# A pre-norm transformer block in f32: attention by two heads and 512 queries on tiled TensorE, projections a block behind

## Chip, cores and metric

The kernel runs on one core of a Trainium2 chip. The metric is the device time of one execution in microseconds (us), given as the median of several runs. The engines are called as in the profile: PE is TensorE (PEld its weight loads), DVE is VectorE, ACT is ScalarE, POOL is GpSimd and SP is SyncE, which here only issues DMAs.

## What is computed

`x` has shape (2, 1024, 1024): batch, tokens, features. All data is f32, there are 32 heads of 32 features, and the feed-forward width is 2752. Cut to what matters:

```python
def attn(x):
    qkv = x @ attn_qkvw + attn_qkvb               # heads of 32 features
    scores = einsum('bhqd,bhkd->bhqk', q, k) / sqrt(32)
    probs = softmax(scores, axis=-1)
    ctx = einsum('bhqk,bhkd->bhqd', probs, v)
    return ctx @ attn_ow + attn_ob
def ffn(x):
    return (silu(x @ W_gate.T) * (x @ W_up.T)) @ W_down.T
x = x + attn(layernorm(x))
x = x + ffn(layernorm(x))
```

## The kernel before

The tokens of a batch entry (S = 1024) are eight key tiles of 128 (NT) and two blocks of 512 (NS). The work has these stages: layer norm and transposes of `x` (line 259); projections of queries and keys (`qk_steps`, matmul at L366) and of values (`v_steps`, L422), whose results go to DRAM; attention by head (class `Head`); then, per block of 512 tokens, the output projection (`oproj_steps`, L711) and the feed-forward network (`ffn_steps`). The last uses the seven-product scheme for the gate and up projections (L853, 256 columns each) and for most of the down projection (L994); the sums of weights that it needs are made once by GpSimd (`weight_sum_steps`, L1105).

Attention of one head: queries and keys were stored as a rounded high part (`hi`, L379, f32r) and the rest (`lo`, L381). `load` (L465) brings them as 128 rows: for queries high, low, each twice; for keys each row in pairs, so that one f32r matmul of 128 rows forms all products of the parts. `scores(kt)` (L490) does two of these, for one key tile and all 1024 queries, into a PSUM tile `s` of two banks (two such buffers). ScalarE copies it to an SBUF tile `p` (L502), VectorE keeps a running maximum `top` over key tiles (L505, L507). `maximum` (L511) reduces it over the 128 keys and sends it through DRAM to all partitions as `m`. `less_maximum` (L545) adds the negative maximum to `p`, on GpSimd for six of eight key tiles and VectorE for two. `exponential` (L548) is ScalarE's. `values(kt)` (L550) multiplies `p` by `vones`, which are the 32 features of the values beside 32 columns of ones, so that contexts and softmax sums arise together: two matmuls of 64 weight columns, the first 512 queries into PSUM rows 0 to 63 and the second into rows 64 to 127. They come in runs of four key tiles (RUN). `finish` copies `acc` and stores contexts and sums to DRAM; `prep_ctx` takes reciprocals and multiplies contexts by them, on GpSimd (L660).

What sets the order is a planner, the class `Emitter` (L44). Steps carry costs in planner nanoseconds (`MM4` = 855 for an f32 matmul of 512 columns, `MM1` = 230 for an f32r one). `run(fill, paced, side)` takes steps of two lists: a paced step marked as a beat goes out when it is due, beats being spread evenly over the cost of both lists, and fill steps stand between; a step can need a mark that another gives, and `later` puts off a step by planner time (loads, stores and the maximum's way through DRAM use it). Side steps go out as soon as their needs are met. Each engine executes its instructions in the order in which they are emitted.

Attention's beats are key tiles: at beat `n` the scores of tile `n`, the subtraction of tile `n-10`, the exponential of tile `n-11` and, every fourth beat, four `values` up to tile `n-12`. `p` has RING = 16 buffers. The main part (L1206 to L1219) makes two long lists: the first runs 32 heads and two more heads' scores beside the projections of both batch entries (`fill`), the second runs the rest beside the last projections (`keep_qk`) and the output projection and feed-forward network of batch entry 0 (`ffn0`). The feed-forward network of entry 1 (`ffn1`) has no attention beside it. Thirty matmuls are cut from the end of `ffn0` (`keep`) and run after attention has ended.

Of the kernel before, what the change touches and what calls it, by code (L numbers as in the profile page):

```python
# [130 lines left out]
def preln_block_kernel(  # L131
# [28 lines left out]
    MM4, MM1 = 855.0, 230.0  # L160
    QTR = 4
    LAG = 2
    RUN = 4
    RING = NT + LAG + RUN + 2
# [44 lines left out]
    def dtile(shape, name):  # L209
        return dram.tile(shape, F32, tag=name, name=name)  # L210

    dq = {
        (b, g, w): dtile([P, 2, S], f"dq{b}_{g}_{w}")
        for b in range(B)
        for g in range(G)
        for w in range(2)
    }
    dv = {(b, hf): dtile([S, NH], f"dv{b}_{hf}") for b in range(B) for hf in range(NHF)}
    dctx = {(b, i): dtile([H // QTR, S], f"dctx{b}_{i}") for b in range(B) for i in range(QTR)}
    dsum = {(b, i): dtile([HEADS // QTR, S], f"dsum{b}_{i}") for b in range(B) for i in range(QTR)}  # L220
    drec = {(b, i): dtile([HEADS // QTR, S], f"drec{b}_{i}") for b in range(B) for i in range(QTR)}

# [128 lines left out]
    def qk_steps(q, b, g, halves=None):  # L351
# [5 lines left out]
        def store(w, s, hl, part):  # L357
            rows = dq[b, g, w][:, hl, s * NH : (s + 1) * NH]
            nc.sync.dma_start(rows, part.bitcast(F32))

        def project(w, s, kc):
            if kc == 0:
                qk_ps[w, s] = lps(f"pq_{b}_{g}_{w}_{s}")
            ps = qk_ps[w, s]
            hk, k = divmod(kc, KC // 2)
            nc.tensor.matmul(  # L366
                ps,
                wqk[b, g, w, hk][:, k, :],
                xnT[b, s][:, kc, :],
                start=(kc == 0),  # L370
                stop=(kc == KC - 1),
            )
            if s == NS - 1 and k == KC // 2 - 1:
                wst.next()
            if kc < KC - 1:
                return
            bias = bqk_t[:, w * G + g : w * G + g + 1]
            hi = Sm(f"hi_{b}_{g}_{w}_{s}", F32R)
            nc.scalar.activation(hi, ps, AF.Identity, bias=bias, scale=1.0)  # L379
            lo = Sm(f"lo_{b}_{g}_{w}_{s}", F32R)  # L380
            nc.vector.scalar_tensor_tensor(lo, ps, bias, hi.bitcast(F32), ALU.add, ALU.subtract)  # L381
            last = w == 1 and s == NS - 1
            em.later(4000.0, lambda: store(w, s, 0, hi))
            em.later(5500.0, lambda: store(w, s, 1, lo), ("qk", b, g) if last else None)
# [61 lines left out]
    vones = [const.tile([P, NT, 2, HD], F32, tag=f"vones{i}", name=f"vones{i}") for i in range(2)]  # L446
    for t in vones:
        nc.gpsimd.memset(t[:, :, 1, :], 1.0)
# [5 lines left out]
    class Head:  # L454
# [3 lines left out]
        def __init__(self, b, h):  # L458
            self.b, self.h, self.g = b, h, h // HPG
            self.hf = self.g // (G // NHF)  # L460
            self.name = f"{b}_{h}"
            self.v = vones[(b * HEADS + h) % 2]
            self.p = {}

        def load(self, i):  # L465


            if i == 0:
                self.qk = [
                    att.tile([P, S], F32R, tag=tag, bufs=2, name=f"{tag}_{self.name}")  # L470
                    for tag in ("qs", "ks")
                ]
            r = (self.h % HPG) * HD
            src = dq[self.b, self.g, min(i, 1)][r : r + HD, :, :]
            if i == 0:
                twice = bass.AP(src.tensor, src.offset, [[S, 2 * HD], [0, 2], [1, S]])
                nc.scalar.dma_start(self.qk[0].bitcast(F32), twice)
            else:
                part = src[:, i - 1, :]
                twice = bass.AP(part.tensor, part.offset, [part.ap[0], [0, 2], part.ap[1]])  # L480
                nc.scalar.dma_start(self.qk[1][i - 1 :: 2, :].bitcast(F32), twice)

        def load_v(self):
            c = (self.h * HD) % NH
            nc.sync.dma_start(
                self.v[:, :, 0, :],
                dv[self.b, self.hf][:, c : c + HD].rearrange("(c p) n -> p c n", p=P),
            )

        def scores(self, kt):  # L490
            q, k = self.qk
            ps = psum.tile([P, S], F32, tag="s", bufs=2, name=f"s_{self.name}_{kt}")
            for s in range(NS):
                nc.tensor.matmul(  # L494
                    ps[:, s * NH : (s + 1) * NH],
                    k[:, kt * P : (kt + 1) * P],
                    q[:, s * NH : (s + 1) * NH],
                    start=True,
                    stop=True,
                )  # L500
            p = self.p[kt] = Pt(f"p_{self.name}_{kt}")
            nc.scalar.copy(p, ps)  # L502
            if kt == 1:
                self.top = att.tile([P, S], F32, tag="top", bufs=1, name=f"top_{self.name}")
                nc.vector.tensor_tensor(self.top, ps, self.p[0], ALU.max)  # L505
            elif kt > 1:
                nc.vector.tensor_tensor(self.top, ps, self.top, ALU.max)  # L507
            if kt == NT - 1:
                self.maximum()

        def maximum(self):  # L511
# [15 lines left out]
            def turn():  # L527
# [11 lines left out]
                ("max", self.b, self.h),  # L539
            )  # L540

        def less_maximum(self, kt):
            p = self.p[kt]
            eng = nc.vector if kt % 4 == 3 else nc.gpsimd
# [4 lines left out]

        def values(self, kt):  # L550

            if kt == 0:
                self.acc = psum.tile([P, NH], F32, tag="acc", bufs=1, name=f"acc_{self.name}")
            for s in range(NS):
                nc.tensor.matmul(  # L555
                    self.acc[s * 2 * HD : (s + 1) * 2 * HD, :],
                    self.v[:, kt, :, :].rearrange("p a n -> p (a n)"),
                    self.p[kt][:, s * NH : (s + 1) * NH],
                    start=(kt == 0),
                    stop=(kt == NT - 1),  # L560
                )
# [3 lines left out]
        def finish(self):  # L565
            part, n = divmod(self.h, HEADS // QTR)
            cs = Sm(f"cs_{self.name}")
            nc.scalar.copy(cs, self.acc)

            def store(s):  # L570
                r = 2 * s * HD
                cols = slice(s * NH, (s + 1) * NH)
                nc.sync.dma_start(
                    dctx[self.b, part][n * HD : (n + 1) * HD, cols], cs[r : r + HD, :]
                )
                nc.sync.dma_start(dsum[self.b, part][n : n + 1, cols], cs[r + HD : r + HD + 1, :])

            em.later(2500.0, lambda: store(0))
            em.later(2600.0, lambda: store(1), ("ctx", self.b, self.h))

    def attention_steps(cut):


        heads = [Head(b, h) for b in range(B) for h in range(HEADS)]
        lists = [Steps(), Steps()]
        total = len(heads) * NT
        q = lists[0]

        def load_step(k, i):
            if k < len(heads):  # L590
                q.add(lambda: heads[k].load(i), needs=("qk", heads[k].b, heads[k].g))

        for i in range(3):
            load_step(0, i)
        for n in range(total + NT + LAG + 2):
            if n == cut:
                q = lists[1]
            k, kt = divmod(n, NT)
            if n < total:
                if kt % 2 == 0 and kt < 6:  # L600
# [4 lines left out]
                if kt == NT - 2:  # L605
                    q.add(heads[k].load_v, needs=("v", heads[k].b, heads[k].hf))
                q.add(lambda k=k, kt=kt: heads[k].scores(kt), 2 * MM1, beat=True)
# [3 lines left out]
            if 0 <= k < len(heads):  # L611
                needs = ("max", heads[k].b, heads[k].h)
                q.add(lambda k=k, kt=kt: heads[k].less_maximum(kt), needs=needs)
            k, kt = divmod(n - NT - LAG - 1, NT)
            if 0 <= k < len(heads):
                q.add(lambda k=k, kt=kt: heads[k].exponential(kt))
            k, kt = divmod(n - NT - LAG - 2, NT)
            if 0 <= k < len(heads) and kt % RUN == RUN - 1:
                for v in range(kt - RUN + 1, kt + 1):
                    q.add(lambda k=k, v=v: heads[k].values(v), MM4)  # L620
# [5 lines left out]
    def prep_ctx(b):  # L626


        def recip(i):
            cols = HEADS // QTR * S // P  # L630
            sm = small([P, cols], "sums", 1, f"sums_{b}_{i}")
            flat = lambda d: d.rearrange("h s -> (h s)").rearrange("(p c) -> p c", p=P)
            nc.sync.dma_start(sm, flat(dsum[b, i]))
            rc = small([P, cols], "recs", 1, f"recs_{b}_{i}")

            def go():
                nc.vector.reciprocal(rc, sm)
                nc.sync.dma_start(flat(drec[b, i]), rc)

            em.later(7000.0, go, ("rec", b, i))  # L640
# [4 lines left out]
        def load(blk, i):  # L645
            cols = slice(blk * NH, (blk + 1) * NH)
            n = KC // QTR
            part = ctxT[b, blk][:, i * n : (i + 1) * n, :]
            nc.sync.dma_start(part, dctx[b, i][:, cols].rearrange("(g p) n -> p g n", p=P))
            recs = [Sm(f"rec_{b}_{blk}_{i}_{g}") for g in range(n)]  # L650
            for g, rec in enumerate(recs):
                for j in range(HPG):
                    nc.sync.dma_start(
                        rec[j * HD : (j + 1) * HD, :],
                        drec[b, i][g * HPG + j, cols].partition_broadcast(HD),
# [9 lines left out]
        per = HEADS // QTR  # L665
        recips, loads = Steps(), Steps()
        for i in range(QTR):
            recips.add(lambda i=i: recip(i), needs=("ctx", b, (i + 1) * per - 1))
        for blk in range(NS):
            if blk > 0:  # L670
# [4 lines left out]
            for i in range(QTR):  # L675
                if i > 0:
                    loads.add(lambda: None, needs=("mult", b, blk, i - 1))
                loads.add(lambda blk=blk, i=i: load(blk, i), needs=("rec", b, i))
# [388 lines left out]
    def weight_sum_steps():  # L1067
        q = Steps()

        def start(i):  # L1070
# [42 lines left out]
            for j, args in enumerate(todo):  # L1113
                em.later(9500.0 + 3500.0 * j, lambda args=args: add(*args))
                em.later(19000.0 + 2500.0 * j, lambda j=j: store(j), ("ws", i) if j == 3 else None)
# [12 lines left out]
    with tc.manual_schedule():  # L1128
# [71 lines left out]
        def tail(q, b):  # L1200
            for blk in range(NS):
                st = {}
# [68 lines left out]
```

## Time and profile before

| | |
|---|---|
| median of 3 runs | 3320.51 us (3315.83 to 3322.61) |
| profiled execution | 3320.87 us |
| its span, first to last instruction | 3319.1 us |
| granted TensorE clock, mean | 0.995 of full |
| score matmuls (L494), 128 x 512 | 1024 instructions, 467.0 us busy |
| value matmuls (L555), 64 columns of weights | 2048 instructions, 468.2 us busy |
| L545 subtraction, GpSimd / VectorE | 384 at 2444 ns / 128 at 1426 ns |
| L548 exponential / L502 copy, ScalarE | 512 at 1060 ns / 512 at 1010 ns |
| L507 maximum, VectorE | 384 at 1222 ns |
| L381 `lo`, VectorE | 64 at 747 ns |

The page lists busy time by engine, then groups of instructions by line with their mean duration. An f32 matmul of the program is two PE instructions, an f32r matmul one. PE durations contain the pipeline's length and overlap; the time from the start of one matmul to the start of the next says how long the array was taken. In the timeline a row is a stretch of like instructions: start, length, engine, line, operation, shape and count; a bracket at its end is the idle time before it and what ended it. A row of waits is: who waited, for whom, microseconds in total, times, longest.

### The profile page before, as it was taken

How to read it: one execution, taken by the hardware profiler on the slowest of the kernel's cores; microseconds unless marked ns; L12 is line 12 of the kernel's file. 1: busy time of each engine (PE TensorE's matmuls, PEld its weight loads, DVE VectorE, ACT ScalarE, POOL GpSimd, SP SyncE). 2: the span in 40 equal slices, each digit the busy share in tenths (PEclk: the TensorE clock that was granted, in tenths of full speed). 3: DMA queues.
4: the chain of work that ended last, by engine and by line, in shares of the span. 5: the costliest groups of instructions: out<-in, count | busy, mean ns of one | idle time of the engine just before them, and what ended most of it. 6: DMA issues, size and time to landing. Idle time of an engine off the chain costs nothing.

```text
span 3319.1 us, 34091 instructions
## 1 busy us (share of the span) xinstructions
PE 3246.9 (98%) x11456; PEld 1883.5 (57%) x11456; DVE 1767.1 (53%) x2454; ACT 1358.8 (41%) x1520; POOL 1187.0 (36%) x584
## 2 busy tenths in 40 slices
PE   8999998999999999999999999999999999999999
PEld 4444343444444446666664566666557777476775
DVE  3455555555555466666656675566434333344434
ACT  2465565656666455555563555555200000010000
POOL 0377666666775543333335333333210000200000
PEclk9999998999999999999999999999999999999999
DMA  4665665566555635555555455554545555645553
GB/s 166 198 210 175 204 219 183 161 211 203 191 191 168 200 108 151 154 157 153 152 164 181 127 153 158 155 154 138 166 159 153 153 153 149 196 143 152 154 153 96
DMA packets 336702, 548.64 MB, mean 165 GB/s; under 512 B 104976, under 2 KB 104976, under 8 KB 336528
## 3 DMA queue, kind: packets, MB, share of 16 engines
q1 hardware_dynamic: 281360, 414.31, 41.1%
q10 hardware_dynamic: 55168, 132.15, 12.2%
q8 instruction: 92, 1.51, 0.2%
q14 instruction: 82, 0.67, 0.1%
HBM read 454.30 MB, written 92.01 MB: 165 GB/s over the span
## 4 chain that ended last, share of the span: by engine, by line
PE 81%; DMA 6%; DVE 3%; POOL 3%; ACT 3%; issue 2%; ACTq 0%; SPq 0%; POOLq 0%; DVEq 0%
PE p L853 30%; PE pd L994 14%; PE acc L555 10%; PE pq L366 7%; PE po L711 6%; PE s L494 5%; PE pvv L422 5%; DMA m<-d 2%; POOL p L545 2%; PE pd L926 2%; DMA d<-neg 2%; ACT p L502 1%; POOL ws L1105 1%; DVE top L507 1%; PE pg L897 1%
## 5 line engine op out<-in xcount | busy, mean ns | idle before, releaser
L545 POOL TENSOR_TENSOR p<-p,m 128x1024 f32<-128x1024 f32 x384 | 928.4, 2444 | 995.3 <-DMA m<-d 717.7
L502 ACT COPY p<-s 128x1024 f32<-128x1024 f32 x512 | 516.9, 1010 | 630.7 <-PE s L494 595.9
L507 DVE TENSOR_TENSOR top<-s,top 128x1024 f32<-128x1024 f32 x384 | 469.1, 1222 | 551.1 <-ACT p L502 548.5
L548 ACT ACTIVATE p<-p 128x1024 f32<-128x1024 f32 x512 | 542.1, 1060 | 251.4 <-POOL p L545 236.8
L853 PE MATMUL p<-sum,m 128*128 128x256 f32 x2688 | 610.5, 381 | 2.7 <-DVE sum L764 1.9
L853 PEld LDWEIGHTS p<-sum,m 128*128 128x128 f32 x2688 | 508.6, 190 | 92.0 <-issue 15.2
L494 PE MATMUL s<-qs,ks 128*128 128x512 f32 x1024 | 467.0, 537 | 22.8 <-DVE top L507 22.8
L366 PE MATMUL pq<-xnT,wqk 128*128 128x512 f32 x1024 | 469.6, 596 | 0.0
L555 PE MATMUL acc<-p,vones 128*64 128x512 f32 x2048 | 468.2, 599 | 0.5 <-ACT p L548 0.4
L853 PE MATMUL p<-xn2T,m 128*128 128x256 f32 x2016 | 464.7, 380 | 0.7 <-DVE gate L876 0.7
L994 PE MATMUL pd<-wp,h 128*128 128x512 f32 x960 | 429.3, 594 | 0.2
L853 PEld LDWEIGHTS p<-xn2T,m 128*128 128x128 f32 x2016 | 380.0, 190 | 73.9 <-issue 17.0
L494 PEld LDWEIGHTS s<-qs,ks 128*128 128x128 f32 x1024 | 186.5, 191 | 233.8 <-issue 147.1
L994 PEld LDWEIGHTS pd<-wp,h 128*128 128x128 f32 x960 | 180.1, 190 | 214.3 <-issue 192.4
L366 PEld LDWEIGHTS pq<-xnT,wqk 128*128 128x128 f32 x1024 | 194.4, 191 | 187.4 <-issue 175.0
L555 PEld LDWEIGHTS acc<-p,vones 128*64 128x64 f32 x2048 | 135.3, 136 | 267.7 <-issue 211.4
L1007 DVE TENSOR_TENSOR x<-pd,x 128x512 f32<-128x512 f32 x360 | 236.8, 684 | 83.3 <-PE pd L994 83.3
L916 POOL MEMSET h<- 64x512 f32 x4 | 2.1, 524 | 678.1 <-PE pd L994 678.1
L881 ACT ACTIVATE gate<-gate 128x512 f32<-128x512 f32 x84 | 52.9, 630 | 464.5 <-DVE gate L880 464.3
L422 PE MATMUL pvv<-wv,xnT 128*128 128x512 f32 x512 | 236.8, 600 | 1.5 <-ACT xnT L267 0.9
L711 PE MATMUL po<-wo,ctx 128*128 128x512 f32 x512 | 227.6, 594 | 0.0
L545 DVE TENSOR_TENSOR p<-p,m 128x1024 f32<-128x1024 f32 x128 | 182.5, 1426 | 0.0
(90 smaller groups left out, 2049.4 us busy)
## 6 DMA issues: line engine op xcount, KB each, us to landing
m<-dws SPq DMA_DIRECT2D x336, 256.0 KB
m<-in_w_gu SPq DMA_DIRECT2D x252, 256.0 KB
wp<-ddn SPq DMA_DIRECT2D x160, 256.0 KB
qs<-dq ACTq DMA_DIRECT2D x64, 512.0 KB
ks<-dq ACTq DMA_DIRECT2D x128, 256.0 KB
m<-d SPq DMA_DIRECT2D x64, 512.0 KB
wp<-in_w_dn SPq DMA_DIRECT2D x120, 256.0 KB
raw<-in_w_gu ACTq DMA_DIRECT2D x84, 256.0 KB
```

Of the source, the lines that this page charges most:

```text
L366: nc.tensor.matmul(ps, wqk[b, g, w, hk][:, k, :], xnT[b, s][:, kc, :], start=(kc == 0), stop=(kc == KC - 1),)
L422: nc.tensor.matmul(st["ps"], xnT[b, t // TB][:, kc, (t % TB) * P : (t % TB + 1) * P], st["w"][kc], start=(kc == 0), stop=(kc == KC - 1),)
L494: nc.tensor.matmul(ps[:, s * NH : (s + 1) * NH], k[:, kt * P : (kt + 1) * P], q[:, s * NH : (s + 1) * NH], start=True, stop=True,)
L502: nc.scalar.copy(p, ps)
L507: nc.vector.tensor_tensor(self.top, ps, self.top, ALU.max)
L545: eng.tensor_tensor(p, p, self.m, ALU.add)
L548: nc.scalar.activation(self.p[kt], self.p[kt], AF.Exp, scale=SCALE)
L555: nc.tensor.matmul(self.acc[s * 2 * HD : (s + 1) * 2 * HD, :], self.v[:, kt, :, :].rearrange("p a n -> p (a n)"), self.p[kt][:, s * NH : ( ...
L711: nc.tensor.matmul(st["ps"], ctxT[b, blk][:, g, t * P : (t + 1) * P], st["w"][hf, g], start=(g == 0), stop=(g == G - 1),)
L853: nc.tensor.matmul(ps, mats[c, n][:, kc, :], rhs, start=(kc == 0), stop=(kc == hk - 1),)
L994: nc.tensor.matmul(st["pd"], lefts[n](pi)[:, j, t * P : (t + 1) * P], st["wp", pi, n, j], start=(j == 0), stop=(j == PART // 2 - 1),)
L1007: nc.vector.tensor_tensor(xs, st["pd"], xs, op)
```

## The change

Attention is done by units of two heads and one block of 512 queries, so a unit's `p` tiles are still 128 x 1024 (two heads side by side) and there are 64 units. The order is batch entry, block of queries, pair of heads.

- Queries and keys are stored and used as f32, without high and low parts; `lo` is gone. Each is loaded twice, to rows 0 to 63 and 64 to 127, keys so that even key tiles lie in the first half and odd ones in the second.
- `scores(i)` does two key tiles at once: four matmuls of 32 rows of the array each (two key tiles by two heads), with 128 weight columns and 512 moving columns, into the four banks of both `s` buffers. It goes out on every second beat.
- New: `differences` (GpSimd) replaces the values of even key tiles by the difference to the odd tile after; `add` (VectorE in the first phase; later VectorE and GpSimd by turns) adds the exponentials of an even tile to those of the odd tile. So the ones need only odd tiles.
- `values(kt)` does four matmuls of 32 weight columns and 256 moving columns, into 32 PSUM rows each (two heads by two halves of the queries), and for odd tiles four more with ones.
- The values follow one beat later, `p` has 18 buffers, and after the first phase the subtraction is GpSimd's for seven of eight tiles.
- Contexts, sums and reciprocals are kept per block. Each block's output projection and feed-forward network are a list of their own (`rest`), and run beside the attention of the next block; the last thirty matmuls of each list move into the next.
- The steps within a weight sum stand closer in planner time.

The core of the diff:

```diff
-    RING = NT + LAG + RUN + 2
+    RING = NT + LAG + RUN + 4
...
-            hi = Sm(f"hi_{b}_{g}_{w}_{s}", F32R)
-            nc.scalar.activation(hi, ps, AF.Identity, bias=bias, scale=1.0)
-            lo = Sm(f"lo_{b}_{g}_{w}_{s}", F32R)
-            nc.vector.scalar_tensor_tensor(lo, ps, bias, hi.bitcast(F32), ALU.add, ALU.subtract)
+            vec = Sm(f"qk_{b}_{g}_{w}_{s}")
...
-                twice = bass.AP(src.tensor, src.offset, [[S, 2 * HD], [0, 2], [1, S]])
-                nc.scalar.dma_start(self.qk[0].bitcast(F32), twice)
...
+            r = self.j * 2 * HD
+            rows = slice(i * 2 * HD, (i + 1) * 2 * HD)
+            q = dq[self.b, self.g][r : r + 2 * HD, self.blk * NH : (self.blk + 1) * NH]
+            nc.scalar.dma_start(self.q[rows, :], q)
+            nc.scalar.dma_start(self.k[rows, :], dk[self.b, self.g][r : r + 2 * HD, i, :])
...
-            for s in range(NS):
-                nc.tensor.matmul(
-                    ps[:, s * NH : (s + 1) * NH],
-                    k[:, kt * P : (kt + 1) * P],
-                    q[:, s * NH : (s + 1) * NH],
-                    start=True,
-                    stop=True,
-                )
...
+            kts = (2 * i, 2 * i + 1)
+            ps = [
+                psum.tile([P, S], F32, tag="s", bufs=2, name=f"s_{self.name}_{kt}") for kt in kts
+            ]
+            for a in range(2):
+                for h in range(2):
+                    rows = slice((2 * a + h) * HD, (2 * a + h + 1) * HD)
+                    nc.tensor.matmul(
+                        ps[a][:, h * NH : (h + 1) * NH],
+                        self.k[rows, i * P : (i + 1) * P],
+                        self.q[rows, :],
+                        start=True,
+                        stop=True,
+                    )
...
-            eng = nc.vector if kt % 4 == 3 else nc.gpsimd
+            own = kt % 4 == 3 if self.phase == 0 else kt == NT - 1
+            eng = nc.vector if own else nc.gpsimd
...
+        def differences(self):
+
+            v = self.v.rearrange("p (i a) n -> p i a n", a=2)
+            nc.gpsimd.tensor_tensor(v[:, :, 0, :], v[:, :, 0, :], v[:, :, 1, :], ALU.subtract)
+
+        def add(self, kt):
+
+            eng = nc.vector if self.phase == 0 or kt % RUN == RUN - 1 else nc.gpsimd
+            eng.tensor_tensor(self.p[kt], self.p[kt], self.p[kt - 1], ALU.add)
...
-            for s in range(NS):
-                nc.tensor.matmul(
-                    self.acc[s * 2 * HD : (s + 1) * 2 * HD, :],
-                    self.v[:, kt, :, :].rearrange("p a n -> p (a n)"),
-                    self.p[kt][:, s * NH : (s + 1) * NH],
-                    start=(kt == 0),
-                    stop=(kt == NT - 1),
-                )
+
+            def columns(w, c, start, stop):
+                for j in range(HPG):
+                    part, h = divmod(j, 2)
+                    q0 = h * NH + part * NQ
+                    nc.tensor.matmul(
+                        self.acc[j * HD : (j + 1) * HD, c : c + NQ],
+                        w(h),
+                        self.p[kt][:, q0 : q0 + NQ],
+                        start=start,
+                        stop=stop,
+                        skip_group_check=True,
+                    )
+
+            v = lambda h: self.v[:, kt, h * HD : (h + 1) * HD]
+            columns(v, 0, kt == 0, kt == NT - 1)
+            if kt % 2 == 1:
+                columns(lambda h: ones, NQ, False, kt == NT - 1)
...
-                em.later(9500.0 + 3500.0 * j, lambda args=args: add(*args))
-                em.later(19000.0 + 2500.0 * j, lambda j=j: store(j), ("ws", i) if j == 3 else None)
+                em.later(8500.0 + 3000.0 * j, lambda args=args: add(*args))
+                em.later(16000.0 + 2500.0 * j, lambda j=j: store(j))
+            em.later(19500.0, lambda: None, ("ws", i))
...
+        def rest(n):
+
+            q, late, st = Steps(), Steps(), {}
+            b, blk = divmod(n, NS)
+            turn = oproj_steps(q, b, blk, st)
+            ffn_steps(q, b, blk, st, turn)
+            while late.cost < 30 * MM4:
+                late.items.insert(0, q.items.pop())
+            return q, late
+
+
+        rests = [rest(n) for n in range(B * NS)]
+        lists = attention_steps([(n + 1) * UNITS * NT + 2 * NT for n in range(B * NS - 1)])
+        side = [*prep_ctx(0), *prep_ctx(1)]
         em.run(head)
-        em.run(fill, first, side=(*prep0, weight_sum_steps()))
-        em.run(joined([keep_qk, ffn0]), second, side=(*prep0, *prep1))
-        em.run(keep, side=prep1)
-        em.run(ffn1, side=prep1)
+        em.run(fill, lists[0], side=(*side, weight_sum_steps()))
+        keep = keep_qk
+        for (q, late), beats in zip(rests, [*lists[1:], None]):
+            em.run(joined([keep, q]), beats, side=side)
+            keep = late
+        em.run(keep)
         em.settle(True)
```

## The prediction

> **What bounds the kernel now.** I read the page's busy table and groups first, then the busy times by stretch, then the waits, and last the timeline of TensorE over a few microseconds. The page opens with:
>
> ```profile
> span 3319.1 us, 34091 instructions
> ...
> PE 3246.9 (98%) x11456; PEld 1883.5 (57%) x11456; DVE 1767.1 (53%) x2454; ACT 1358.8 (41%) x1520; POOL 1187.0 (36%) x584
> ```
>
> TensorE is busy 98% of the span; no other engine passes 53%. By stretch (head left out: attention beside projections, attention beside the first feed-forward, feed-forward alone), the columns being length, then busy time of PE, PEld, DVE, ACT, POOL:
>
> ```profile
> 90.00:1010.00 920.00, 878.10 (x2751) 387.99 (x2751) 516.40 (x552) 554.15 (x601) 614.62 (x308) 0.99 0.61 195
> 1010.00:2385.00 1375.00, 1360.09 (x5108) 819.77 (x5105) 841.39 (x1138) 728.30 (x783) 534.61 (x239) 1.00 0.51 154
> 2385.00:3319.00 934.00, 929.13 (x3380) 636.05 (x3378) 383.27 (x706) 55.92 (x109) 36.56 (x30) 1.00 0.50 152
> ```
>
> TensorE lacks work for 42, 15 and 5 us of these. The waits of the first stretch name VectorE's running maximum, which holds the score buffers:
>
> ```profile
> PE s L494 <- DVE top L507: 20.0, 13, 3.5
> PE top L529 <- DVE part L518: 6.7, 8, 1.3
> ```
>
> So about 60 us could be won by pacing; anything more must come from fewer TensorE microseconds. What it spends is read from the timeline (start, length, line, count), in order of time:
>
> ```profile
> 1497.32 1.03 PE L853 MATMUL p<-xn2T,m 128*128 128x256 f32 x4
> 1497.99 0.81 PE L494 MATMUL s<-qs,ks 128*128 128x512 f32 x2
> 1498.73 3.65 PE L555 MATMUL acc<-p,vones 128*64 128x512 f32 x16
> 1502.31 1.56 PE L853 MATMUL p<-xn2T,m 128*128 128x256 f32 x6
> 1503.52 0.82 PE L494 MATMUL s<-qs,ks 128*128 128x512 f32 x2
> ...
> 1504.18 3.18 PE L853 MATMUL p<-xn2T,m 128*128 128x256 f32 x14
> 1507.20 1.46 PE L853 MATMUL p<-sum,m 128*128 128x256 f32 x6
> 1508.31 0.81 PE L494 MATMUL s<-qs,ks 128*128 128x512 f32 x2
> 1508.96 3.40 PE L853 MATMUL p<-sum,m 128*128 128x256 f32 x15
> ```
>
> Lengths overlap, so I use starts. Fourteen `p` of 256 columns fill 1504.18 to 1507.20: 0.216 us each. An f32 matmul is two such instructions. From 1507.20 to 1508.96 stand six `p` (1.30) and two `s`: 0.46 for the pair, so one f32r score matmul takes 0.23. The `acc` run is the key row: 16 instructions of 512 columns, 0.43 each when alone, start at 1498.73 and the next at 1502.31, 3.58 us, not 6.9. The weight loads show why:
>
> ```profile
> 1499.21 0.14 PEld L555 LDWEIGHTS acc<-p,vones 128*64 128x64 f32 x2 [0.29 <-issue]
> 1499.64 0.14 PEld L555 LDWEIGHTS acc<-p,vones 128*64 128x64 f32 x2 [0.29 <-issue]
> 1500.07 0.14 PEld L555 LDWEIGHTS acc<-p,vones 128*64 128x64 f32 x2 [0.29 <-ACT p L502]
> ```
>
> They come in pairs every 0.43 us: the two column tiles already run fully side by side, each loading its next weights under the running pair.
>
> **Price of a change of tiling.** Eight slots of 0.429 are 3.43 of the 3.58. From 1497.32 to 1498.73 four `p` and two `s` need 1.32 and take 1.41. From 1502.31 to 1504.18 six `p` and two `s` need 1.76 and take 1.87. So one excursion into column tiles costs 0.15 + 0.09 + 0.11, some 0.34 us. The single starts in the trace split it: 94 ns empty at each change, and a first weight load that nothing hides, 51 ns for 64 columns going in, 105 ns for 128 going out. I take 94 ns plus the load in proportion: 0.20 us into 128-column weights, 0.12 into 32-column ones.
>
> **Values.** Before: 64 heads by 2 runs, each 8 × 0.429 + 0.34 = 3.78, ×128 = 483 us. After: a run of four key tiles has four groups with the values and two with the ones (pairs of exponentials added first), each two slots of 256 columns on four tiles: 12 × 0.2155 + 0.12 in + 0.20 out = 2.91, ×128 = 372. Gain 111 us. Four tiles side by side are not in the trace; two are, without loss. Bounds: 372 if they overlap as two do, about 700 if only two of four do. I take the first, the nearest row.
>
> **Scores.** Before: 512 × 0.461 = 236 us; they need no change of tiling. After: 64 × 4 groups, each four row tiles in two slots of 0.429 = 0.858, entered at 0.20. Half of them stand right before a values run (both fall due on the same beats), so the way out is already counted there; 128 return to the full array at 0.20. That is 256 × 1.06 + 26 = 297 us. Loss 61 us: 17 won by the array time, 78 lost to changes of tiling. Bounds: about 219 if row tiles take their weights without an empty array, and 379 if the four 128-column loads of a group go one after another (3 × 0.107 more for each of 256 groups, 82 us). I take 297, from the `acc` row, where the loads of two tiles start 6 ns apart.
>
> Two rules of the Trainium skill bear on this. "TensorEngine Tiling (Array Packing)", Key Properties: a change of tiling mode drains the array, while different tiles load and multiply in parallel. It names no price; by the planner's own costs (no price at all) the change would give 125 us, by the trace's it gives 50. "TensorE: Matmul & The Clock Gate", Part 3, measured only 3.07 times from four row tiles of 512 columns. As a loss in every group that would be 4 × 0.858/3.07 = 1.12 rather than 0.858, an estimate of 67 us more, and the change would be nearly worthless; but the trace's two column tiles reach twice the rate but for entry and exit, and one group with entry and exit (1.26) is already only 2.7 times. I read the 3.07 as such ends and add nothing.
>
> **Work off TensorE.** The exponentials' additions: 256 of 128×1024. VectorE takes 16×4 + 48×2 = 160 at 1.43 (the L545 row on VectorE) = 228 us and gives up 48 subtractions (69) and 64 `lo` (48): +111 on 1767. GpSimd per unit: 6 × 2.44 + about 0.65 for the differences (half of the 1.28 of a 512-element sum) = 15.3 in the first phase, 7 + 2 operations + 0.65 = 22.6 later; 16 × 15.3 + 48 × 22.6 = 1330 against 939 before. Cover: a later phase has one feed-forward block, about half of the 934 us stretch, plus a quarter of all attention, (372 + 297)/4 = 167: some 630 us for 16 units, 39 us each. GpSimd has 22.6 of that, ScalarE 8 × 2.07 and about 4 for the rest; VectorE 11.6 of maximum, 4.3 of subtraction and additions, and 383/2/16 = 12 of feed-forward, 28 in all, 72% (67% before). All fit, so I cost the additions at nothing. Without that cover, the next `values` waits one addition, 2.44 us.
>
> **Moved and queued.** The first stretch now carries 16 units instead of 32 heads: fewer copies and maxima per microsecond, while the weight sums (124 × about 1.4 us on GpSimd) come closer together, and a raw load on ScalarE's queue that waits for GpSimd would hold the copies behind it, hence the next score group. That group now needs both score buffers at once, but comes every second beat (about 9 us) and the two copies and maxima take 2 × 1.0 and 2 × 1.2. ScalarE issues 4 query and key loads per unit instead of 3, about 0.5 us each, of half the bytes; SyncE stores 64 q/k tiles instead of 128, two context stores per unit instead of four, and 8 more loads and stores of sums and reciprocals. None bounds. Ring slots for exponentials rise with the later values (18 against 16), so that reuse keeps two beats. Each block's projections wait for its own contexts, but 30 matmuls held back from the block before, with attention between, lie ahead (over 30 us), against about 22 us from last context to ready; at nothing. Of the 57 us idle in the attention stretches I take 15 as saved. Bounds: 45 saved, 40 more lost.
>
> **Sum.** Profiled execution 3320.9 us (span 3319.1 and 1.8 around it; the median of the runs is 3320.5, the same for this purpose). −111 + 61 − 15 = −65, so 3256 us.
>
> **Rivals.**
> - *Row tiles load their weights in turn (slower).* Then every score group starts 0.32 us later: +82, 3338 us. It decides from 0.25 us extra per group, where the gain is gone. For it: no row tile is in the trace, and each tile here loads all 128 columns. Against: two column tiles load together.
> - *Changes of tiling are mostly hidden.* If the next tile's loads run ahead of the drain, the 78 us fall away: 3180. Against: the `acc` rows pay each time.
> - *New waits.* VectorE at 72%, additions before values, paired score buffers and closer weight sums give back 40 us instead of saving 15: 3311. Speaking for it: L507 is the only engine wait of weight now.
> - *It does not do what it says.* If four tiles overlap only in twos, values cost about 330 more and scores 220 more: some 3800. Against: the clean overlap of two.
>
> **Numbers.** Likeliest 0.53, alone 3225 to 3295; loads in turn 0.18; new waits 0.12; hidden changes 0.11; no fourfold overlap 0.06. Range 3190 to 3345. A measurement of this kernel can tell about 0.2% from no change. Faster 0.71 (likeliest 0.53, hidden 0.11, new waits 0.07), same 0.05, slower 0.24 (0.16 of loads in turn, 0.06, 0.02).
>
> **What would show it.** In the changed profile: starts of the values' matmuls in fours a few ns apart, groups every 0.216 us; scores in fours, 0.43 us apart, with 0.2 us empty ahead of each; weight loads of a score group within some 20 ns of each other, not 107 apart; 640 changes of tiling instead of 256; the wait of scores for `top` no longer than 20 us. The forecast is wrong if score groups take over 1.4 us of TensorE, or if TensorE's idle time grows.

## The result and the profile after

The changed kernel takes 3494.1 us (3489.3 to 3497.1, 4 runs), 1.0527 times the kernel before (95% interval 1.0509 to 1.0545): 5.3% slower, where 2% faster was forecast, and 149 us beyond the upper end of the range. The page of the kernel after, span and busy times:

```profile
span 3487.5 us, 44233 instructions
...
PE 3270.6 (94%) x16576; PEld 1829.1 (52%) x16576; DVE 2011.6 (58%) x2510; ACT 1407.3 (40%) x1570; POOL 1638.7 (47%) x791
```

TensorE's share fell from 98% to 94%, though the span grew. By stretch, columns as in the prediction (attention beside projections, beside the first, second and third feed-forward blocks, and the last block alone):

```profile
90.00:855.00 765.00, 744.01 (x3518) 313.41 (x3517) 416.25 (x382) 335.40 (x372) 469.88 (x248) 0.99 0.59 182
855.00:1490.00 635.00, 589.70 (x3323) 340.54 (x3322) 400.58 (x494) 305.65 (x336) 347.12 (x158) 0.98 0.44 132
1490.00:2220.00 730.00, 666.41 (x3768) 392.93 (x3767) 476.24 (x593) 351.91 (x383) 397.27 (x180) 0.96 0.45 133
2220.00:2990.00 770.00, 702.49 (x3971) 414.52 (x3970) 491.50 (x615) 364.73 (x395) 402.86 (x184) 0.96 0.44 131
2990.00:3487.00 497.00, 489.14 (x1785) 328.66 (x1783) 203.92 (x374) 29.27 (x56) 20.75 (x17) 1.00 0.47 147
```

Beside the projections and in the last block TensorE is nearly full; beside the feed-forward blocks it lacks 45, 64 and 68 us, with VectorE busy only 63% to 65% of the time. TensorE's waits in the kernel after (who waited for whom, total, times, longest):

```profile
PE pd L1038 <- DVE x L1051: 53.2, 34, 3.7
PE top L546 <- DVE part L535: 35.8, 25, 7.0
PE p L897 <- DVE up L917: 17.7, 8, 2.9
```

Before, the score matmuls waited for their buffers; now the feed-forward matmuls wait for VectorE to take their results. The second row is of another kind: the transpose `top`, which turns the reduced maximum on TensorE, waits for VectorE's reduction itself, and all that stands behind it in TensorE's queue waits with it. Added up from the starts of all matmuls (every gap of over 0.15 us beyond a matmul's own slot and a change of tiling), TensorE's waits are 84 us before and 292 after: +208. By such a count some 200 of the 292 stand before feed-forward matmuls and 52 before `top`, against 17 and 10 before. The executions that were profiled differ by 3489 - 3321 = 168 us, so TensorE's own work fell by about 40; 50 was forecast.

That work went as forecast. The timeline of TensorE in the kernel after:

```profile
1700.22 1.14 PE L510 MATMUL s<-q,k 32*128 32x512 f32 x8
1701.29 1.07 PE L588 MATMUL acc<-p,vals 128*32 128x256 f32 x16
1702.18 0.61 PE L588 MATMUL acc<-p,ones 128*32 128x256 f32 x8
1702.61 1.05 PE L588 MATMUL acc<-p,vals 128*32 128x256 f32 x16
1703.47 0.61 PE L588 MATMUL acc<-p,ones 128*32 128x256 f32 x8
1704.02 0.66 PE L258 MATMUL pt_f<-ident,xn 128*128 128x128 f32 x4
...
1709.34 1.14 PE L510 MATMUL s<-q,k 32*128 32x512 f32 x8
1710.41 0.92 PE L897 MATMUL p<-xn2T,m 128*128 128x256 f32 x3
```

A values run lasts from 1701.29 to 1704.02: 48 instructions in 2.73 us, twelve slots with four tiles abreast, against sixteen instructions in 3.58 before. A score group takes 1.07 us from 1709.34 to 1710.41, eight instructions in two slots; single starts show the four tiles 7 ns apart, their weight loads too.

### The profile page after: what moved, and what is told of

Read it like the earlier page. It is cut to its first block, busy times and chain, and to the rows that moved or that the text cites. A ratio compares the mean times of both kernels' runs of the same rounds, so it can differ in the third digit from the quotient of the medians.

```text
span 3487.5 us, 44233 instructions
## 1 busy us (share of the span) xinstructions
PE 3270.6 (94%) x16576; PEld 1829.1 (52%) x16576; DVE 2011.6 (58%) x2510; ACT 1407.3 (40%) x1570; POOL 1638.7 (47%) x791
## 5 line engine op out<-in xcount | busy, mean ns | idle before, releaser
L563 POOL TENSOR_TENSOR p<-p,m 128x1024 f32<-128x1024 f32 x432 | 1068.8, 2499 | 45.7 <-DMA m<-d 43.6
L519 ACT COPY p<-s 128x1024 f32<-128x1024 f32 x512 | 493.3, 1015 | 1005.8 <-PE s L510 921.6
L576 POOL TENSOR_TENSOR p<-p,p 128x1024 f32<-128x1024 f32 x96 | 231.3, 2409 | 905.5 <-ACT p L566 873.5
L897 PE MATMUL p<-xn2T,m 128*128 128x256 f32 x2016 | 482.5, 390 | 37.2 <-DVE up L917 17.7
L1038 PE MATMUL pd<-wp,h 128*128 128x512 f32 x960 | 453.9, 618 | 54.7 <-DVE x L1051 47.8
L510 PE MATMUL s<-q,k 32*128 32x512 f32 x2048 | 298.0, 651 | 0.0
L588 PE MATMUL acc<-p,vals 128*32 128x256 f32 x4096 | 273.2, 385 | 0.0
L576 DVE TENSOR_TENSOR p<-p,p 128x1024 f32<-128x1024 f32 x160 | 263.6, 1648 | 0.0
L1149 POOL TENSOR_TENSOR ws<-raw 128x512 f32<-128x512 f32 x62 | 85.6, 1381 | 328.7 <-DMA raw<-in_w_gu 223.5
L588 PEld LDWEIGHTS acc<-p,vals 128*32 128x32 f32 x4096 | 120.4, 110 | 167.2 <-issue 95.0
```

The source lines that it names most:

```text
L510: nc.tensor.matmul(ps[a][:, h * NH : (h + 1) * NH], self.k[rows, i * P : (i + 1) * P], self.q[rows, :], start=True, stop=True,)
L519: nc.scalar.copy(p, s)
L563: eng.tensor_tensor(p, p, self.m, ALU.add)
L576: eng.tensor_tensor(self.p[kt], self.p[kt], self.p[kt - 1], ALU.add)
L588: nc.tensor.matmul(self.acc[j * HD : (j + 1) * HD, c : c + NQ], w(h), self.p[kt][:, q0 : q0 + NQ], start=start, stop=stop, skip_group_chec ...
L897: nc.tensor.matmul(ps, mats[c, n][:, kc, :], rhs, start=(kc == 0), stop=(kc == hk - 1),)
```

## Where the waits come from

The timeline of VectorE in the kernel after, beside a feed-forward block; a score group went out on TensorE at 2010.00:

```profile
2012.28 2.55 DVE L524 TENSOR_TENSOR top<-s,top 128x1024 f32<-128x1024 f32 x2 [2.17 <-ACT p L519]
2014.93 0.71 DVE L534 STREAM_TRANSPOSE m<-top 128x512 f32<-128x512 f32 x1
2015.68 0.69 DVE L535 TENSOR_REDUCE part<-m 128x16 f32<-128x512 f32 x1
2016.29 0.70 DVE L534 STREAM_TRANSPOSE m<-top 128x512 f32<-128x512 f32 x1
2017.02 0.69 DVE L535 TENSOR_REDUCE part<-m 128x16 f32<-128x512 f32 x1
2017.62 0.41 DVE L917 TENSOR_TENSOR up<-p,gate 128x256 f32<-128x256 f32 x1
```

of ScalarE:

```profile
2011.23 1.93 ACT L519 COPY p<-s 128x1024 f32<-128x1024 f32 x2 [3.62 <-PE s L510]
```

and of TensorE:

```profile
2010.00 1.14 PE L510 MATMUL s<-q,k 32*128 32x512 f32 x8
2011.07 5.02 PE L897 MATMUL p<-sum,m 128*128 128x256 f32 x22
2018.09 2.53 PE L897 MATMUL p<-xn2T,m 128*128 128x256 f32 x6 [2.01 <-DVE up L917]
```

VectorE stands still in its queue for 2.17 us, while TensorE makes the scores and ScalarE copies the first tile (2011.23 to 2012.24; the copy of the second, done at 2013.16, is in time for its maximum). Then it does both maxima and at once the reduction of the last pair: 7.5 us from 2010.1 to 2017.6 in which it takes no other result. TensorE has three buffers for results, of eight instructions at 0.216 = 1.72 us each, so about 5 us later it stops, here for 2.0 us. In the kernel before the same piece was one copy, one maximum and the reduction: 1.0 + 1.2 + 2.8 = 5.0 us, about what is covered. (In the traces that last piece, standing still included, has a median of 5.5 us before and 7.2 us after, beside the feed-forward network.) So the theory A: *long pieces of VectorE's queue*. Rivals: B and C, the load that the additions put on VectorE; D, the new arrangement of the blocks.

## Experiments

All are compared with the kernel before on the same chip. "Waits" are TensorE's, added up as above, in the profiled execution.

**e1: odd maxima a beat later.** In `scores` the maximum of the odd tile is left out; a step `odd_maximum` at the next beat does it, and the reduction after the last.

```diff
+            self.odd = ps[1]
...
                 q.add(lambda: None, beat=True)
+                if n < total:
+                    q.add(lambda k=k, kt=kt: units[k].odd_maximum(kt))
```

> The kernel after, but the running maximum of the odd key tile of each pair (and the reduction that follows the last one) goes to VectorE one beat later. Theory A (paired scores make VectorE wait for two copies and then work on two maxima, with the reduction 7.5 us in one piece, while the feed-forward results behind it hold TensorE's three PSUM buffers): pieces shrink to about 4 us, most of the 290 us of TensorE's waits go; 3330 us, at most 3400. Theory B (VectorE is simply overloaded by additions, and slowed beside GpSimd): no work is taken away, so within 20 us of 3494.

Measured 3385.1 us (ratio 1.0183, 1.0155 to 1.0212), waits 159. No work was taken away and 109 us went: A, not B, though short of the 3330 us that A was given.

**e2: the reduction in two halves.** `em.later(3000.0, ...)` and `em.later(6000.0, ...)` for its halves; what follows them 3 us later.

> The kernel after, but the reduction of the maximum is put off in two halves by 3 and 6 us of planner time (and the steps after it by 3 us). Theory A: the longest piece falls from 7.5 to 4.7 us and only every fourth pair was that long; half of the waits go, about 3370 us. Theory B: within 20 us of 3494.

Measured 3376.4 us (1.0172, 1.0150 to 1.0194), waits 178, as A expects. Of these, 60 stand before the transpose `top`, which was planned too soon after the later half.

**e3: subtractions and additions of the later phases all on GpSimd.**

```diff
-            own = kt % 4 == 3 if self.phase == 0 else kt == NT - 1
+            own = kt % 4 == 3 if self.phase == 0 else False
...
-            eng = nc.vector if self.phase == 0 or kt % RUN == RUN - 1 else nc.gpsimd
+            eng = nc.vector if self.phase == 0 else nc.gpsimd
```

> The kernel after, but in the later phases all subtractions and additions of the exponentials are GpSimd's (VectorE loses one subtraction and two additions per unit, about 5.3 us with the slowing beside GpSimd). Theory A: the pieces of copies and maxima stay; VectorE is free sooner after them, 3440 to 3480 us. Theory B: VectorE's load falls by 250 us in the stretches that stall, waits fall by more than half: below 3380 us. If GpSimd becomes late instead (29 us of work per unit), slower than 3494.

Measured 3475.7 us (1.0461, 1.0446 to 1.0477), waits 283. VectorE was relieved, but 53 us of the waits now stand before the values, which wait for GpSimd. Within A's expectation, and no proof by itself: relief and lateness are mixed.

**e4: the kernel before, with paired scores.** At even beats `[heads[k].scores(t) for t in (kt, kt + 1)]`, nothing at odd ones.

> The kernel before, but the scores of two key tiles are emitted together on every second beat; nothing else is changed and no work added. Theory A: VectorE gets the same long pieces as in the kernel after, and beside the feed-forward network (30 heads) 2 to 4 us are lost per head, as many per head beside the projections or fewer: 3380 to 3450 us. Theory B: the same load, so 3318 within 15 us.

Measured 3356.9 us (1.0097, 1.0080 to 1.0114), waits 119 instead of 84. Pairing alone costs 35 us with the same work: the direction of A, but less than the 60 to 130 expected. I had carried over the loss per unit of the kernel after. And most of the new waits are not of the kind that A describes:

```profile
PE top L529 <- DVE part L518: 33.0, 15, 10.8
PE pd L995 <- DVE x L1008: 10.7, 10, 3.7
```

They stand before `top`, which waits for the late reduction (33 us against 7 in the kernel before), and few before feed-forward matmuls whose buffers are full. The last pieces are as long here (7.0 us in the median) as in the kernel after. Why that kernel loses three times as much per piece stays open; e13 shows that the additions are not the reason.

**e5: e1 and e2 together** (halves at 2.5 and 5 us, transpose at 8.5).

> The kernel after with both measures of the first two runs: odd maxima a beat later, and the reduction in two halves 2.5 and 5 us after them. Theory A (long pieces on VectorE): they removed about 109 and 118 us of 176 to be had; together the longest piece is about 2.5 us, waits of TensorE near 100 us: 3310 us, between 3280 and 3345. Theory C (what is left comes from the additions and the slower VectorE beside GpSimd): the second measure adds little, 3345 to 3375.

Measured 3327.0 us (12 runs; 1.0016, 1.0003 to 1.0030), waits 123. The long pieces account for 3494 - 3327 = 167 us. Both kinds of wait shrink:

```profile
PE pd L1047 <- DVE x L1060: 16.6, 13, 3.6
PE top L553 <- DVE part L539: 14.5, 9, 3.0
```

VectorE between two score groups of e5:

```profile
2019.72 1.22 DVE L522 TENSOR_TENSOR top<-s,top 128x1024 f32<-128x1024 f32 x1 [2.02 <-ACT p L520]
2020.86 0.41 DVE L926 TENSOR_TENSOR up<-p,gate 128x256 f32<-128x256 f32 x1
2021.84 0.42 DVE L928 TENSOR_TENSOR up<-p,up 128x256 f32<-128x256 f32 x1 [0.57 <-PE p L906]
2022.18 0.41 DVE L929 TENSOR_TENSOR gate<-p,gate 128x256 f32<-128x256 f32 x1
2022.51 1.21 DVE L528 TENSOR_TENSOR top<-s,top 128x1024 f32<-128x1024 f32 x1
2023.64 2.65 DVE L583 TENSOR_TENSOR p<-p,p 128x1024 f32<-128x1024 f32 x1
```

Three feed-forward results are taken between the maxima. The piece that is left is the addition, 2.65 us here.

**e6: e5 without differences and additions.** Both operations are dropped, and `columns(ones)` runs for every key tile.

> The kernel of the run with both measures, without differences and additions of exponentials; the ones are multiplied for every key tile. Computes the same. TensorE pays 64 x 4 more groups of ones, two slots of 0.2155 each: +110 us. Theory A: the additions cost little in waits, so about 90 to 110 us slower than that run. Theory C: 60 us or more of waits go with the additions, so at most 50 us slower.

Measured 3374.3 us (1.0167, 1.0152 to 1.0182), waits 61 instead of 123: the additions cost 62 us of waits. TensorE pays 110 us more, and the time grows by only 47. C, for this part. VectorE's and GpSimd's additions go at once here, so the run does not tell whose they are.

**e7: the kernel after with attention in two halves, as before.** One cut after 32 units; the second half runs beside both feed-forward blocks of entry 0.

> The kernel after, but attention in two halves as before: batch entry 0 beside all projections, entry 1 beside both feed-forward blocks of entry 0, none beside the others. Theory A: the long pieces are a loss per unit beside feed-forward (about 5 us each); 30 such units instead of 46, but closer together: waits of 170 to 280 us, 3380 to 3480 us. Theory D (the arrangement a block behind is itself the loss): TensorE's waits fall to the about 90 us of the kernel before, 3260 to 3290 us.

Measured 3525.0 us (1.0624, 1.0607 to 1.0642), waits 293. Slower than the kernel after, and the waits are nowhere near D's 90 us: D falls. It is above A's range too; in the first stretch 32 units beside the projections now stall as well, the second 16 of them with the later split of work, in which GpSimd has seven of eight subtractions. The waits are those of the kernel after, but the score groups now wait for their second buffer:

```profile
PE s L510 <- DVE top L524: 41.2, 35, 4.2
```

Of 512 score slots 90 come apart into two tiles and two (2 in the kernel after), each up to 0.43 us longer, which the sum of waits does not count.

**e8: e5 with the last subtraction on GpSimd too.**

> The kernel of the run with both measures, and in the later phases the last of eight subtractions moves from VectorE to GpSimd too. Theory A: one piece of 1.4 to 3.2 us per unit less on VectorE, 10 to 30 us faster than that run. If GpSimd, then at 25 us per unit, is late for the values: equal or slower.

Measured 3342.5 us (1.0070, 1.0055 to 1.0085): slower, as the second half of the expectation has it; waits 150, 13 of them before the values.

**e9: e5 with even maxima 2.5 us later,** so that VectorE need not stand behind ScalarE's copies.

> The kernel with both measures (odd maxima a beat later, reduction in two halves), and the maximum of the even key tile put off by 2.5 us of planner time, so that VectorE no longer stands still in its queue until ScalarE has copied the scores (508 us of such standing still there). Theory A: what is left of TensorE's waits (123 us) is partly results behind this wait; 20 to 50 us go: 3280 to 3305 us, faster than the kernel before. Theory C (only the load of the additions is left): within 10 us of 3327.

Measured 3337.3 us (1.0050, 1.0032 to 1.0068). A's gain misses, and C's "within 10 us" is missed by a fraction of a microsecond: VectorE stood still 366 instead of 508 us, and TensorE's waits rose to 147. Less standing still ahead of short pieces gained nothing here.

**e10: e9 with the reduction and the transpose 2 us sooner.**

> The same, with the two halves of the reduction at 1.5 and 3.5 us after the last maximum instead of 2.5 and 5, and what follows them 2 us sooner, so that the maximum reaches GpSimd as early as in the kernel after. Theory A: the pieces stay short; GpSimd's 280 us of waiting for the maximum shrink, and with them the rare long waits (13.5 us at a block's end) of the chain subtraction, exponential, copy, maximum: 0 to 20 us faster than the run before it in this list. If the two halves come too close to the last maximum again: slower by up to 20 us.

Measured 3365.7 us (1.0134, 1.0119 to 1.0149), waits 166, of which 46 stand before the transpose. Slower than e9 by 28, more than the 20 expected; 19 of it are waits, and e12 shows a further cause.

**e11: e5 with the transpose 1.5 us later.**

> The kernel with both measures, and the transpose that turns the maximum on TensorE 5 us instead of 3.5 us of planner time after the last half of the reduction (16 us of TensorE's waits there stood in front of this transpose, 46 us in the run that left it 3 us). If TensorE, which takes its work in order, waits there because VectorE is behind the planner: 5 to 15 us faster than 3327. If the later maximum holds up subtractions and values instead: equal or slower.

Measured 3350.2 us (1.0087, 1.0072 to 1.0103). The waits before the transpose did fall, from 16 to 4 us, but GpSimd's waits for the maximum rose from 280 to 408 us, and TensorE's waits in all to 152.

**e12: e5 with the last pair of maxima together, transpose at 11 us.**

> The kernel with both measures, but the last pair of maxima of a unit stays together, so that the reduction can begin a beat sooner (halves at 3 and 6 us, the transpose at 11 us, the maximum still 2 us sooner than before for GpSimd). Theory A: one longer piece (4.7 us, about what TensorE's three buffers cover) per unit, but no waits in front of the transpose and fewer of GpSimd for the maximum: 0 to 25 us faster than 3327. If the longer piece counts: slower by 10 to 30 us.

Measured 3365.6 us (1.0148, 1.0131 to 1.0165): 39 us slower than e5, above the 10 to 30 expected. Not all of it is the longer piece: by the same count the waits are about 150, 28 more than in e5. The other part is a collision on TensorE:

```profile
2808.74 0.61 PE L597 MATMUL acc<-p,vals 128*32 128x256 f32 x8
2809.29 0.33 PE L555 MATMUL top<-ident,part 128*128 128x128 f32 x1
2809.55 0.64 PE L597 MATMUL acc<-p,vals 128*32 128x256 f32 x8
```

The transpose `top` stands inside the values run, so TensorE leaves the column tiles and comes back: 0.81 us between the starts of the two groups of values, of which their two slots are 0.43 and the transpose itself 0.11, so some 0.27 us are lost. That happens in 57 of 64 units here, in 59 of e1 and e10, 47 of e6, 29 heads of e4, but in 2 of e5 and e9 and in none of the kernel after and e11. At 0.27 us it is 15 us of e12's and e10's difference, an estimate.

**e13: the kernel after without differences and additions,** which completes the square.

> The kernel after, unchanged in its paired maxima and undivided reduction, but without differences and additions; the ones are multiplied for every key tile. Computes the same. TensorE pays 110 us more in matmuls. With the long pieces taken apart, the additions cost 62 us of TensorE's waits (123 against 61). If the two causes simply add (long pieces alone leave 292 - 62 = 230 us of waits): 3494 + 110 - 62 = 3542 us. If the long pieces hurt only because the additions and their slowing beside GpSimd leave VectorE no time to catch up: waits of 100 to 150 us, 3420 to 3460 us. If the additions hardly matter while pieces are long: 3590 us or more.

Measured 3532.1 us (1.0642, 1.0621 to 1.0663), waits 225: the two causes simply add.

| waits of TensorE, us | with additions | without |
|---|---|---|
| pieces long | 292 (after) | 225 (e13) |
| pieces short | 123 (e5) | 61 (e6) |

Long pieces cost 169 or 164 us of waits, additions 67 or 62. No version here is faster than the kernel before; e5 comes within 0.03% to 0.30% of it. Why e5's neighbours e9 to e12 are 10 to 39 us slower is told only in part: a gain before one instruction came back before another, in e10 and e12 `top` fell into the values runs, and no run here isolates more than that.

## Why the prediction was wrong

*Values and scores: right.* A values run was forecast at 2.91 us with both changes of tiling; measured 0.11 + 2.73 + 0.105 = 2.94. A score group that returns to the full array was put at 1.26; measured from single starts 0.094 + 1.07 + 0.105 = 1.27. Changes of tiling cost what was put down for them, and there are 644 against 640 forecast. The loss in every group that I had weighed because of the 3.07 did not come: four tiles lose nothing but entry and exit. Row tiles load together, so the rival of loads in turn is refuted.

*"All fit, so I cost the additions at nothing": this step failed,* with "none bounds" for the paired scores. I compared busy time with available time over a whole unit. VectorE's load was near what I reckoned: 1368 us beside the feed-forward network, 29.7 for each of 46 units against 28. As a share it was even lower (64% against 72%), because each unit took 46 us instead of 39. (The 67% given for the kernel before does not come out of its trace, which has 841 of 1375 us there, 61%.) Yet TensorE waited 2 us here and 3 there. What e1, e2 and e5 show in place of the load is the length of one stretch in VectorE's in-order queue: results queue behind it, and three buffers cover about 5 us of that; the transpose `top`, which no buffer covers, waits for its end. I had the terms (2 x 1.0, 2 x 1.2, the reduction) but asked only whether they fit into two beats, not who is queued behind them. That is 167 us.

*The additions' size.* I took 1.43 us each from the L545 row. That mean hid two populations. In the kernel before, VectorE's 128x1024 subtraction takes 1.21 us when GpSimd does not work on SBUF at the same time (80 of 128) and 1.78 when it does; in the kernel after the additions take 1.21 and 2.27 (66 of 160 beside GpSimd). Their waits cost 62 to 67 us against nothing forecast. On balance they still pay: without them TensorE has 110 us more of matmuls.

*Waits: the sign was wrong.* I took 15 us as saved and bounded the loss at 40; it was 208. With some 10 us of work that TensorE did not save, that is the whole way from the forecast 3256 us to the 3489 of the profiled execution: 208 + 15 + 10 = 233. The rival of new waits named the right place and a fifth of its size. The fewer copies and maxima per microsecond help only beside the projections, where little is lost; beside the feed-forward 46 units met a VectorE that has TensorE's results to take every 1.7 us.

*Half clock.* Part of the 208 is a consequence. After a wait of 3.49 us that began near 2060.4 in the kernel after, the stretches 2060 to 2072 show (PE and the granted clock, third from the end):

```profile
2060.00:2064.00 4.00, 0.67 (x3) 0.14 (x1) 3.93 (x7) 0.00 (x0) 0.00 (x0) 0.86 0.21 67
2064.00:2068.00 4.00, 3.87 (x6) 1.28 (x6) 4.00 (x7) 0.00 (x0) 0.00 (x0) 0.50 0.17 44
2068.00:2072.00 4.00, 4.00 (x16) 1.48 (x20) 2.01 (x4) 0.03 (x1) 0.00 (x0) 0.78 0.28 88
```

The three rows come to some 7 us at half clock, and the matmuls in them start 0.85 us apart instead of 0.43. The mean granted clock of the run is 0.978 against 0.995. Matmuls at half rate make 48 of the 292 us of waits, against 10 of 84 before, and 15 of 123 in e5. "TensorE: Matmul & The Clock Gate" of the Trainium skill, Part 1, has the two rates, and an idle window of about 3.4 us behind which the half rate stands; this spell agrees.

## What to carry to other kernels

When work is moved onto an engine that also empties another's buffers, compare its longest uninterrupted stretch with the time that those buffers cover; its mean load does not show that. (How far standing still ahead of a stretch counts, no run here isolates.) Then look for an instruction in the other engine's own queue that needs the end of the stretch: no buffer covers that one. Emit such work in pieces shorter than the cover, with the other engine's results between them. When two narrow matmuls are merged to save TensorE time, look at what their results start on the next engine all at once.

## What the runs showed of the hardware

Four row tiles of 512 columns and four column tiles of 256 run abreast without loss, in slots of 0.429 and 0.216 us. A change of tiling empties the array for 94 ns (88 behind the row tiles), after which the first weight load stands open, 105 ns for 128 columns and 24 for 32.

VectorE and GpSimd hold each other up where VectorE reads two operands from SBUF. Lines of the kernel after, GpSimd and then VectorE at the same moment:

```profile
2029.52 2.36 POOL L576 TENSOR_TENSOR p<-p,p 128x1024 f32<-128x1024 f32 x1 [14.21 <-ACT p L566]
```

```profile
2029.71 3.25 DVE L563 TENSOR_TENSOR p<-p,m 128x1024 f32<-128x1024 f32 x1
```

The subtraction that takes 1.21 us alone starts 0.19 us after GpSimd's addition and takes 3.25, 2.0 more, about the rest of the other (2.17). The maxima, which read one operand from PSUM, take 1.22 us with or without GpSimd (318 and 130 of them), and the transposes of `top`, with one operand in SBUF, 0.71 us (32 and 96). "SBUF — State Buffer" of the Trainium skill, in "SBUF: two separate sides", says that a VectorE operation with two SBUF inputs and a GpSimd operation take a shared port pair in turn, each for its whole instruction; the trace agrees in kind and nearly in size. The rule would have told me to price the additions above the L545 mean.
